# Feed-forward blocks that prepare their input early, in a third buffer, beside causal attention on one NeuronCore

## The chip, the cores and the metric

One core of a Trainium2 chip runs the whole program. Its engines are TensorE (PE in the profile, with its weight loads shown apart as PEld), VectorE (DVE), ScalarE (ACT), GpSimd (POOL) and SyncE (SP), which here only issues DMAs. The metric is the device time of one execution in microseconds. Three runs of the kernel before gave a median of 2549.21 us (2546.5 to 2558.14).

## The reference

The input is x of 4096 tokens by 256 features. A causal attention with 16 heads of 16 features works on the normalised and scaled x; its output is added to x and normalised again, which gives x1. Then x1 goes through a feed-forward network with ternary weights (times a scale for each output feature), and the sum of both is normalised once more.

```python
def _L0_ffn_ref(x, w1_w, w1_s, w2_w, w2_s, h1_w, h1_s, h2_w, h2_s, w3_w, w3_s):
    h = jax.nn.silu(_tlin(x, w1_w, w1_s)) * _tlin(x, w2_w, w2_s)   # 256 -> 1024
    h = jax.nn.gelu(_tlin(h, h1_w, h1_s), approximate=False)       # 1024 -> 1024
    h = jax.nn.gelu(_tlin(h, h2_w, h2_s), approximate=False)       # 1024 -> 1024
    return _tlin(h, w3_w, w3_s)                                    # 1024 -> 256
x = L0_attn_x
x = _layernorm(x + _L0_attn_ref(x, L0_attn_gamma, L0_attn_beta, L0_attn_w_qkv))
x = _layernorm(x + _L0_ffn_ref(x, ...))
```

## The kernel before

The 4096 tokens are eight blocks of 512. First come the projections of q, k and v. Then the attention runs over query blocks in the order 0, 1, 2, 3, 4, 6, 7, 5 and, inside each, over four groups of four heads. Every group has two passes over the key blocks. The pass of maxima (`row_max`) multiplies q and k on TensorE (line 411, with the causal mask added by line 418 on the diagonal block) into a two-bank PSUM tile `s`, and VectorE reduces each tile to row maxima (line 422). The pass of scores multiplies again (line 455), ScalarE takes the exponential (line 459), GpSimd zeroes the upper triangle of the diagonal block (line 462), and TensorE multiplies with v into `opsum` (line 473). Both passes share three buffers of `s`.

The feed-forward part of a block ("feed", line 677) starts when the attention of that block is in DRAM, and two feeds, one in each of two slots, are cut into pieces that a hand-written planner (`other`, line 551) puts between the attention's instructions. One call of `other` is a tick of `self.clock`; a tick may give one piece of TensorE work and one deferred step (a "chore": a vector, scalar or GpSimd step of a feed, in one queue, first in, first out). The order of TensorE's instructions is the order in which the planner emits them; the other engines' instructions are ordered by the scheduler of the language. A feed has these stages:

- start (line 643): x is loaded into the slot's own buffer `x1`, the attention's output into the one buffer `at`; GpSimd adds them (line 653), and a layer norm follows in six steps: statistics on VectorE (lines 130 and 131), the inverse root on GpSimd (135, 136), a small product on VectorE (139) and four applications on ScalarE (143).
- transposes of x1 (line 729) and the split of x1 into a high and a low part.
- the gated stage: for each of eight output chunks, two groups of four matmuls (line 748) into the PSUM tile `m`, of which there is one bank. After the first group ScalarE copies it out scaled, `u` (line 751), takes tanh of `u` (753), and VectorE forms (tanh + 1) * u (754). After the second group VectorE multiplies with it (756) and GpSimd splits the result into two parts (700, 701).
- two hidden stages of eight chunks (line 776). ScalarE copies each chunk out into four `raw` buffers (794). At the end of a stage all four get Gelu in one go (705), because the exponential and Gelu need different function tables; for that time the attention does maxima only (`hold`, `saving`). Then GpSimd splits `raw`, two chunks in each chore.
- the last product (line 818), scaled by VectorE into `ys`, which takes the buffer `at` (line 824); GpSimd adds x1 (831), the layer norm follows, and SP writes the block out (834).

Two locks, `at` and `raw`, keep the feeds from holding these buffers at the same time: `at` is taken from the start until x1 is made, and again from the last product until the output is written.

When the attention has ended (line 597 on), what is left of the other feeds runs first. Then comes block 5, the last, alone (the "tail"): eight PSUM banks, splits on VectorE instead of GpSimd, Gelu straight from PSUM (788), and a check that each weight is unchanged by its conversion (`inspect`, line 673), for which SP loads every weight tile again. Its attention never goes to DRAM first: it lies in `final`, and line 649 adds it to x into `at`.

Of the kernel before, what the change touches and what calls it, by code (L numbers as in the profile page):

```python
# [7 lines left out]
F32 = mybir.dt.float32  # L8
FR = mybir.dt.float32r
AF = mybir.ActivationFunctionType  # L10
ALU = mybir.AluOpType
# [36 lines left out]
class Layer:  # L48
# [33 lines left out]
    def run(self):  # L82
        tc, nc, a = self.tc, self.nc, self.a
        with ExitStack() as ctx:
            dram = self.pool(ctx, "dram", space=DRAM)
            cst = self.pool(ctx, "cst")
            self.small = self.pool(ctx, "small", 4)
            self.qaug = [dram.tile([H, 48, B], F32, name=f"qaug{b}") for b in range(NB)]
            self.kaug = [dram.tile([H, KR, B], F32, name=f"kaug{b}") for b in range(NB)]
            self.vaug = [dram.tile([NQ, P, 4, 4, D + 1], F32, name=f"vaug{b}") for b in range(NB)]  # L90
            self.attn = [dram.tile([B, E], F32, name=f"attn{b}") for b in range(NB)]

            self.ident = cst.tile([P, P], F32, name="ident")
            make_identity(nc, self.ident)
            self.mhalf = cst.tile([P, 4], F32, name="mhalf")
            nc.gpsimd.memset(self.mhalf, -0.5)
            self.wbad = cst.tile([P, 22], F32, name="wbad")
            self.wseq = (
                [("glu", g, 0) for g in range(4)]
                + [(n, g, k) for n in ("h1T", "h2T") for g in range(4) for k in range(2)]  # L100
                + [("w3T", 0, k) for k in range(2)]
            )
            self.sc = {}
            for n in ("w1_s", "w2_s", "h1_s", "h2_s"):
                self.sc[n] = cst.tile([P, 8], F32, name=n)
            self.w1_half = cst.tile([P, 8], F32, name="w1_half")
            self.s3 = cst.tile([P, E], F32, name="s3")

            with ExitStack() as fctx, self.in_order(mybir.EngineType.PE):
                self.layer(fctx)  # L110
            bad = self.verdict(cst)
            with tc.If(bad > 0), ExitStack() as gctx:
                self.general(gctx)

    def scales(self):
        for n, t in self.sc.items():
            self.nc.sync.dma_start(t, self.a[n].rearrange("(c p) -> p c", p=P))
        self.nc.gpsimd.tensor_scalar(self.w1_half, self.sc["w1_s"], 0.5, None, ALU.mult)
        s3 = self.a["w3_s"].rearrange("(o f) -> o f", o=1)
        self.nc.sync.dma_start(self.s3, s3.broadcast_to([P, E]))  # L120

    def norm_steps(self, dst, src):
# [18 lines left out]
        def apply(ts):  # L141
# [4 lines left out]
            lambda: stats((0, 1)), lambda: stats((2, 3)), scale, shift, lambda: apply((0, 1)), lambda: apply((2, 3)),  # L146
        )

    def layernorm(self, dst, src):
        for step in self.norm_steps(dst, src):  # L150
            step()

    def defer(self, fn, delay=0, patience=None):

        if self.tail:
            return fn()
        self.asked += 1
        self.chores.append([delay, patience, fn])

    def chore(self, ripe):  # L160
        if self.chores:
            c = self.chores[0]
            if c[0] > 0:
                c[0] -= 1
            elif c[1] is None or ripe or c[1] <= 0:
                self.chores.pop(0)
                c[2]()
                self.did += 1
            else:
                c[1] -= 1  # L170

    def settle(self):

        goal = self.asked
        while self.did < goal and not self.tail:
            yield None, True

    def take(self, what):

        while self.busy[what] and not self.tail:  # L180
            yield None, True
        self.busy[what] = True

    def free(self, what):
        self.busy[what] = False
# [94 lines left out]
    def layer(self, ctx):  # L280
# [22 lines left out]
        self.chores = []  # L303
        self.asked = self.did = 0
        self.busy = {"at": False, "raw": False}
# [8 lines left out]
        def piece():  # L314
# [8 lines left out]
            for _ in range(SLOTS):  # L323
                if not slots[turn] and queue and queue[0] in finished:
                    slots[turn] = self.feed(queue.pop(0), turn)
# [7 lines left out]
            return None, True  # L333

# [134 lines left out]
        def product(qb, qd, kb, t, first, last, pt):  # L469
# [10 lines left out]
            nc.scalar.copy(osb, opsum)  # L480

            def divide():
# [6 lines left out]
                if qb == ORDER[-1]:  # L489
                    if qd == 0:  # L490
                        self.final = self.fk.tile([P, 4, E], F32, name="final")
# [59 lines left out]
        def other():  # L551

            self.clock += 1
            self.chore(len(pending) >= KEEP)
# [42 lines left out]
        spare = next((i for i in range(SLOTS) if not slots[i]), None)  # L597
        if spare is not None:
            self.loaded = self.load(ORDER[-1], spare)
            self.wtiles[spare] = []  # L600
            self.weights(spare, 2)
# [4 lines left out]
        while queue or any(slots):  # L606
            self.clock += 1
            self.chore(True)
            piece()
        if spare is None:  # L610
            spare = 0
            self.loaded = self.load(ORDER[-1], spare)
            self.wtiles[spare] = []
# [5 lines left out]
        for _ in self.feed(ORDER[-1], spare):  # L619
            pass  # L620
# [17 lines left out]
    def load(self, b, slot):  # L638
        x1 = self.fk.tile([P, 4, E], F32, name=f"x1{slot}")
        self.nc.sync.dma_start(x1, tokens(self.a["x"][b * B : (b + 1) * B]))  # L640
        return x1

    def start(self, b, slot, here=False):

        nc, fk = self.nc, self.fk
        x1 = self.loaded if here else self.load(b, slot)
        at = fk.tile([P, 4, E], F32, name="at")
        if here:
            nc.vector.tensor_tensor(at, x1, self.final, ALU.add)
            nc.sync.dma_start(tokens(self.attn[b]), self.final)  # L650
        else:
            nc.sync.dma_start(at, tokens(self.attn[b]))
            self.defer(lambda: nc.gpsimd.tensor_tensor(at, x1, at, ALU.add), 3)
        for step in self.norm_steps(x1, at):
            self.defer(step)
        return x1

# [19 lines left out]
    def feed(self, b, slot):  # L677
# [3 lines left out]
        if not self.tail:  # L681
            self.wtiles[slot] = []

# [27 lines left out]
        def parted(r, h, i):  # L711
            for c in (2 * i, 2 * i + 1):
                split(r[:, c % 2], *(x[:, c % 4] for x in h[c // 4]))
# [4 lines left out]
        yield from self.take("at")  # L718
        x1 = self.start(b, slot, self.tail)
        self.weights(slot, 2)  # L720
        yield from self.settle()
        self.free("at")
        yield from pause(1)
# [13 lines left out]
        for c in range(8):  # L737
# [4 lines left out]
            for i in range(2):  # L742
# [6 lines left out]
                if i == 0:  # L749
                    u = ft.tile([P, B], F32, name="u", bufs=1)  # L750
                    nc.scalar.activation(u, s, AF.Identity, scale=self.w1_half[:, c : c + 1])
                    th = ft.tile([P, B], F32, name="th")
                    nc.scalar.activation(th, u, AF.Tanh)
                    nc.vector.scalar_tensor_tensor(th, th, 1.0, u, ALU.add, ALU.mult)  # L754
                else:
                    nc.vector.scalar_tensor_tensor(th, s, sc["w2_s"][:, c : c + 1], th, ALU.mult, ALU.mult)  # L756
                    split(th, *(x[:, c % 4] for x in h[-1]))
                yield spent(4 * MM, True)
            if self.tail and c % 2:
                self.inspect(c // 2, wt)  # L760
        yield from pause(2)

        for j, sn in ((4, "h1_s"), (12, "h2_s")):
            parts, h = h, []
            yield from self.take("raw")
            if not self.tail:
                raw = [self.fa.tile([P, 2, B], F32, name=f"raw{i}", bufs=1) for i in range(4)]
            for c in range(8):
                g = j + 2 * (c // 2)
# [3 lines left out]
                for k in range(8):  # L773
                    hi, lo = parts[k // 4]
# [6 lines left out]
                if self.tail:  # L781
# [5 lines left out]
                    th = ft.tile([P, B], F32, name="th")  # L787
                    nc.scalar.activation(th, s, AF.Gelu, scale=sc[sn][:, c : c + 1])
                    split(th, *(x[:, c % 4] for x in h[-1]))
                else:  # L790
# [4 lines left out]
                    if c == 7:  # L795
                        self.saving += 1
                        h = [pair(), pair()]
                        self.defer(lambda: gelu(raw), 0, PATIENCE)
                        for i in range(4):
                            self.defer(lambda i=i: parted(raw[i], h, i))  # L800
                yield spent(8 * MM, True)
            if not self.tail:
                self.weights(slot, g + 5)
                yield from self.settle()
            self.free("raw")
            yield from pause(3)

        yield from self.take("at")
        ys = fk.tile([P, 4, E], F32, name="at")
        wts = self.weights(slot, 22)[20:]  # L810
        for u in range(2):
            yp = bank().rearrange("p (t e) -> p t e", e=E)
            for t in range(2):
# [10 lines left out]
            nc.vector.tensor_tensor(  # L824
                ys[:, 2 * u : 2 * u + 2], yp, self.s3.unsqueeze(1).to_broadcast([P, 2, E]), ALU.mult
            )
# [4 lines left out]
        self.defer(lambda: nc.gpsimd.tensor_tensor(ys, ys, x1, ALU.add))  # L831
        for step in self.norm_steps(ys, ys):
            self.defer(step)
        self.defer(lambda: nc.sync.dma_start(tokens(a["out"][b * B : (b + 1) * B]), ys))
        yield from self.settle()
        self.free("at")

    def general(self, ctx):
# [21 lines left out]
        for b in range(NB):  # L860
            x1 = self.start(b, 0)
# [82 lines left out]
```

## Time and profile before

| | |
|---|---|
| median of three runs | 2549.21 us (2546.5 to 2558.14) |
| the profiled execution | 2551.3 us; its span from first to last instruction 2549.6 us |
| PE busy | 2276.0 us, 89% of the span |
| DVE, ACT, POOL busy | 1546.8, 1427.2, 701.6 us |
| mean granted TensorE clock | 0.922 of full speed |
| first feed's transposes / end of the attention / block 5 alone until the end | about 290 us / 2390 us / 2549.6 us |

A row of a group of instructions gives the source line, engine, operation, what it writes and reads with shape and count, then total busy time and mean duration, and then the engine's idle time just before them with what ended it. In a timeline each row is one instruction or a run of equal ones, with start and duration in us; a bracket at its end is the idle time of the engine before it and what ended that. In a list of waits the three numbers are the total in us, how often, and the longest.

### The profile page before, as it was taken

What the parts mean: (1) busy time and instruction counts of PE and PEld (TensorE: products, weight loads), DVE (VectorE), ACT (ScalarE), POOL (GpSimd) and SP (SyncE); (2) the same over time, 40 slices, a digit from 0 to 9 for tenths busy, and PEclk for the clock granted to TensorE, in tenths of its full rate; (3) what the DMA queues carried; (4) which work ended last, traced back from release to release, by engine and by line L of the source; (5) the groups of instructions that cost most, each with busy time, mean ns of one, the idle gap of its engine ahead of it and who ended that gap; (6) DMA issues with size and microseconds to landing.
All of it is one profiled execution on the core that took longest, in us unless ns stands there. A gap on an engine that the chain in (4) does not pass through costs nothing.

```text
span 2549.6 us, 36265 instructions
## 1 busy us (share of the span) xinstructions
PE 2276.0 (89%) x13986; PEld 1222.3 (48%) x13986; DVE 1546.8 (61%) x1795; ACT 1427.2 (56%) x1764; POOL 701.6 (28%) x1008
## 2 busy tenths in 40 slices
PE   4877899998988989999998989999998999999686
PEld 3645345454554543544554534444554534544265
DVE  3544777666757557677656568677655468661263
ACT  3332656555655557556566657666555677667521
POOL 3333222223322134132304033232224132131211
PEclk8777979998998989989999989999999999999888
DMA  7766634533453434534444534444444443443265
GB/s 196 203 162 166 166 101 117 125 105 94 111 135 102 117 99 125 119 88 114 116 120 125 112 85 133 119 111 111 121 109 116 114 128 94 109 111 85 75 169 138
DMA packets 250707, 308.97 MB, mean 121 GB/s; under 512 B 41248, under 2 KB 178592, under 8 KB 250528
## 3 DMA queue, kind: packets, MB, share of 16 engines
q1 hardware_dynamic: 141904, 184.87, 25.3%
q0 software_dynamic: 107264, 119.86, 21.4%
q8 instruction: 113, 1.85, 0.3%
q10 hardware_dynamic: 1360, 1.84, 0.2%
q14 instruction: 66, 0.54, 0.1%
HBM read 267.41 MB, written 38.54 MB: 120 GB/s over the span
## 4 chain that ended last, share of the span: by engine, by line
PE 65%; DVE 13%; issue 6%; ACT 6%; DMA 5%; POOL 5%; SPq 1%; POOLq 0%; ACTq 0%; DVEq 0%
PE m L776 18%; PE opsum L473 16%; PE s L455 11%; PE s L411 10%; DVE mp L422 10%; PE m L748 3%; ACT p L459 3%; PE m L818 2%; PE s L418 1%; PE s L245 1%; POOL act L701 1%; DMA qt<-hl 1%; DVE st L130 1%; DVE th L754 1%; POOL wt L634 1%
## 5 line engine op out<-in xcount | busy, mean ns | idle before, releaser
L422 DVE TENSOR_REDUCE mp<-s 128x2 f32<-128x1024 f32 (+3 forms) x1152 | 1269.0, 1132 | 613.8 <-PE s L411 462.2
L459 ACT ACTIVATE p<-s 128x1024 f32<-128x1024 f32 (+3 forms) x1152 | 1062.7, 955 | 660.1 <-PE s L455 647.6
L455 PE MATMUL s<-qt,sk 50*128 50x512 f32 (+3 forms) x2304 | 514.0, 454 | 83.9 <-DVE mp L422 45.5
L473 PE MATMUL opsum<-p,vk 128*17 128x512 f32 (+3 forms) x4608 | 561.7, 590 | 18.4 <-POOL p L462 13.5
L411 PE MATMUL s<-mk,qt 48*128 48x512 f32 (+3 forms) x2304 | 516.9, 449 | 66.0 <-DVE mp L422 30.8
L776 PE MATMUL m<-act,wt 128*128 128x512 f32 x1792 | 482.7, 412 | 0.2 <-DVE th L756 0.2
L455 PEld LDWEIGHTS s<-qt,sk 50*128 50x128 f32 x2304 | 223.8, 194 | 399.3 <-DVE mp L422 148.8
L776 PEld LDWEIGHTS m<-act,wt 128*128 128x128 f32 x1792 | 324.8, 191 | 126.7 <-issue 54.9
L411 PEld LDWEIGHTS s<-mk,qt 48*128 48x128 f32 x2304 | 230.3, 197 | 319.6 <-ACT p L459 115.1
L473 PEld LDWEIGHTS opsum<-p,vk 128*17 128x17 f32 x4608 | 98.6, 98 | 251.4 <-issue 216.5
L462 POOL TENSOR_SCALAR_AFFINE_SELECT p<-p 128x256 f32<-128x256 f32 x256 | 105.0, 419 | 300.6 <-ACT p L459 299.5
L634 POOL DMA_DIRECT2D wt<-h2T_in x64 | 48.2, 752 | 429.8 <-PE m L776 337.0
L634 POOL DMA_DIRECT2D wt<-h1T_in x64 | 48.9, 764 | 361.8 <-PE m L776 233.0
L701 POOL TENSOR_TENSOR act<-raw,act 128x512 fp32r<-128x512 f32 x112 | 140.1, 1270 | 0.0
L794 ACT ACTIVATE raw<-m,h_s 128x512 f32<-128x512 f32 x112 | 77.1, 688 | 105.1 <-PE m L776 105.1
L748 PE MATMUL m<-xh,wt 128*128 128x512 f32 x224 | 103.2, 461 | 10.3 <-DVE th L756 10.1
L418 PEld LDWEIGHTS s<-tri,pick 64*128 64x128 f32 x1024 | 97.3, 206 | 6.9
L748 PE MATMUL m<-xl,wt 128*128 128x512 f32 x224 | 91.4, 408 | 0.0
L418 PE MATMUL s<-tri,pick 64*128 64x128 f32 (+1 forms) x1024 | 88.8, 252 | 0.0
L776 PE MATMUL bank<-act,wt 128*128 128x512 f32 x256 | 70.3, 432 | 16.2 <-DMA wt<-h2T_in 7.2
L700 POOL CAST act<-raw 128x512 fp32r<-128x512 f32 x112 | 65.2, 609 | 55.6 <-ACT raw L705 55.6
L700 POOL CAST act<-th 128x512 fp32r<-128x512 f32 x56 | 34.3, 613 | 140.5 <-DVE th L756 140.4
(116 smaller groups left out, 1529.9 us busy)
## 6 DMA issues: line engine op xcount, KB each, us to landing
mk<-kaug SPq DMA_DIRECT2D x288, 200.0 KB
sk<-kaug SPq DMA_DIRECT2D x288, 200.0 KB
wt<-h1T_in POOLq DMA_DIRECT2D x64, 512.0 KB, 4.1
wt<-h2T_in POOLq DMA_DIRECT2D x64, 512.0 KB, 5.1
vk<-vaug SPq DMA_DIRECT2D x144, 136.0 KB
qt<-qaug SPq DMA_DIRECT2D x64, 192.0 KB
wt<-w1T_in POOLq DMA_DIRECT2D x32, 256.0 KB, 3.6
wt<-w2T_in POOLq DMA_DIRECT2D x32, 256.0 KB, 5.0
```

The lines of the kernel that those rows point to most:

```text
L411: nc.tensor.matmul(m[:, e, :k1], qt[rows, r, t * P : (t + 1) * P], kt[rows, r, :k1], start=True, stop=kb != qb,)
L418: nc.tensor.matmul(m[:, e, k1 - P + half * i : k1], pick[rows, i], tri[rows, : P - half * i], start=False, stop=i == 1,)
L422: nc.vector.tensor_reduce(mp[:, r, :, t, kb], m[:, :, :k1], AX.X, ALU.max)
L455: nc.tensor.matmul(s[:, e, lo:], kt[rows, r, t * P : (t + 1) * P], qt[rows, r, lo:], start=True, stop=True)
L459: nc.scalar.activation(p[:, :, lo:], s[:, :, lo:], AF.Exp, scale=0.25)
L462: nc.gpsimd.affine_select(out=p[:, :, lo : lo + P], in_=p[:, :, lo : lo + P], compare_op=ALU.is_ge, fill=0.0, base=0, pattern=[[0, 2], [1, ...
L473: nc.tensor.matmul(opsum[32 * j : 32 * j + D + 1, lo:], vt[:, t, j], pt[j // 2][:, j % 2, lo:], start=first, stop=last,)
L634: self.nc.gpsimd.dma_start(dst, src)
L700: eng.tensor_copy(hi, src)
L701: eng.tensor_tensor(lo, src, hi.bitcast(F32), ALU.subtract)
L748: nc.tensor.matmul(s, wt[:, 2 * i + k, cols], x[:, k], start=k == n == 0, stop=k == n == 1)
L776: nc.tensor.matmul(s, wts[k // 4][:, k % 4, cols], x[:, k % 4], start=k == n == 0, stop=k == 7 and n == 1)
```

## The change

Six edits, mostly to the feeds.

1. x1 is made before the feed has a slot. Three buffers of `x1` rotate. A new step `prepare`, called at every tick, starts the next block (`start`) as soon as its attention is there, fewer than three `x1` are in use and `at` is free. The sum is made in place in `x1` by a chore that waits seven ticks, after which `at` is free again; the norm's first and fourth step wait two ticks more each. A slot takes the block when all of this has been emitted.
2. Tanh reads PSUM directly, with the scale folded in; `u` is gone. VectorE's (tanh + 1) * product reads the product from PSUM, and the factor that `u` carried is in a new constant `w12`.
3. Chores are in lanes: one for the next block's preparation and one for each slot. A tick still does one chore, but each lane counts its own delays.
4. The locks `raw0` to `raw3` replace one lock on `raw`; each is freed when its own split is done. A split chore handles one chunk instead of two. The second hidden stage starts when half of the splits have been emitted. The lock `x` covers the split of x1 from the transposes to the end of the gated stage.
5. The last product's two halves are scaled into buffers of `th` (three instead of two) and added to x1 by GpSimd half by half; the norm and the output work in place in `x1`. A slot that is done loads the first two weight tiles of its next block at once.
6. For block 5, `final` is the buffer `at`, and sum and norm (`finish`) are emitted ahead of the tail.

```diff
-    def defer(self, fn, delay=0, patience=None):
+    def defer(self, lane, fn, delay=0, patience=None):
...
+        names = list(self.lanes)
+        turn = self.clock % len(names)
+        for name in names[turn:] + names[:turn]:
...
+            elif done:
+                continue
...
+        def prepare():
+
+            if not project and not self.next and queue and queue[0] in finished and self.live < 3:
+                if "at" not in self.busy:
+                    b = queue.pop(0)
+                    self.next = b, self.start(b)
+            self.more = bool(queue or self.next)
...
-            nc.scalar.copy(osb, opsum)
+            (nc.vector.tensor_copy if self.hold else nc.scalar.copy)(osb, opsum)
...
-    def load(self, b, slot):
-        x1 = self.fk.tile([P, 4, E], F32, name=f"x1{slot}")
+    def load(self, b):
+        self.live += 1
+        x1 = self.fk.tile([P, 4, E], F32, name="x1", bufs=3)
...
+        def total():
+            nc.gpsimd.tensor_tensor(x1, x1, at, ALU.add)
+            self.free("at")
+
+        self.defer("next", total, 7)
+        for delay, step in self.norm_steps(x1, x1):
+            self.defer("next", step, delay)
         return x1
+
+    def reserve(self, slot):
+
+        self.spare = slot
+        self.loaded = self.load(ORDER[-1])
+        self.weights(slot, 2)
+
+    def finish(self):
+
+        self.nc.vector.tensor_tensor(self.loaded, self.loaded, self.final, ALU.add)
+        self.nc.sync.dma_start(tokens(self.attn[ORDER[-1]]), self.final)
+        self.layernorm(self.loaded, self.loaded)
...
-                    u = ft.tile([P, B], F32, name="u", bufs=1)
-                    nc.scalar.activation(u, s, AF.Identity, scale=self.w1_half[:, c : c + 1])
-                    th = ft.tile([P, B], F32, name="th")
-                    nc.scalar.activation(th, u, AF.Tanh)
-                    nc.vector.scalar_tensor_tensor(th, th, 1.0, u, ALU.add, ALU.mult)
+                    th = ft.tile([P, B], F32, name="th", bufs=3)
+                    nc.scalar.activation(th, s, AF.Tanh, scale=self.w1_half[:, c : c + 1])
+                    nc.vector.scalar_tensor_tensor(th, th, 1.0, s, ALU.add, ALU.mult)
                 else:
-                    nc.vector.scalar_tensor_tensor(th, s, sc["w2_s"][:, c : c + 1], th, ALU.mult, ALU.mult)
+                    nc.vector.scalar_tensor_tensor(th, s, self.w12[:, c : c + 1], th, ALU.mult, ALU.mult)
...
-            yield from self.take("raw")
...
+                if not self.tail and c % 2 == 0:
+                    yield from self.take(f"raw{c // 2}")
...
+                    if k % 4 == 0 and c == 0 and j == 12:
+                        yield from self.settle(slot, 4 - k)
...
-                        for i in range(4):
-                            self.defer(lambda i=i: parted(raw[i], h, i))
+                        for i in range(8):
+                            self.defer(slot, lambda i=i, raw=raw, h=h: parted(raw[i // 2][:, i % 2], h, i))
...
-            nc.vector.tensor_tensor(
-                ys[:, 2 * u : 2 * u + 2], yp, self.s3.unsqueeze(1).to_broadcast([P, 2, E]), ALU.mult
-            )
+            ys = ft.tile([P, 2, E], F32, name="th", bufs=3)
+            nc.vector.tensor_tensor(ys, yp, self.s3.unsqueeze(1).to_broadcast([P, 2, E]), ALU.mult)
+            half = x1[:, 2 * u : 2 * u + 2]
+            nc.gpsimd.tensor_tensor(half, half, ys, ALU.add)
...
-        self.defer(lambda: nc.gpsimd.tensor_tensor(ys, ys, x1, ALU.add))
-        for step in self.norm_steps(ys, ys):
-            self.defer(step)
-        self.defer(lambda: nc.sync.dma_start(tokens(a["out"][b * B : (b + 1) * B]), ys))
-        yield from self.settle()
-        self.free("at")
+        for delay, step in self.norm_steps(x1, x1):
+            self.defer(slot, step, delay)
...
+        if self.more:
+            self.weights(slot, 2)
+        elif self.spare is None:
+            self.reserve(slot)
```

## The prediction

> **What bounds the kernel now.** I read the shares first, then the stretches, the waits, and the places on the timeline where those waits stand. TensorE is busy for 2276.0 of 2549.6 us. After the projections (250 us) come two stretches: the attention with the feeds in it, and the tail. Columns: the stretch and its length, busy time of PE, PEld, DVE, ACT and POOL with counts, granted clock, DMA share, GB/s.
>
> ```profile
> 250.00:2390.00 2140.00, 1997.30 (x12567) 1011.79 (x12567) 1357.45 (x1446) 1316.74 (x1577) 589.12 (x815) 0.94 0.45 113
> 2390.00:2549.60 159.60, 108.60 (x462) 84.59 (x462) 76.77 (x148) 29.32 (x46) 23.37 (x28) 0.83 0.50 141
> ```
>
> The middle stretch is TensorE's: 1997.3 of 2140 us, at a clock of 0.94. The matmuls of attention and feeds stay the same in number, so in that stretch the change can only work on the 142.7 us in which TensorE stands, and on the clock. In the tail it stands for 51 us. These are the waits of the middle stretch that the edits touch (total us, times, longest):
>
> ```profile
> PE s L455 <- DVE mp L422: 45.0, 77, 5.9
> PE s L411 <- DVE mp L422: 28.4, 43, 6.8
> PE opsum L473 <- POOL p L462: 13.5, 5, 4.8
> PE m L748 <- DVE th L756: 10.1, 11, 6.1
> DVE st L130 <- POOL at L653: 15.9, 5, 9.9
> DVE st L130 <- POOL at L831: 15.1, 5, 6.8
> ```
>
> "PE waits for line 422" is one name for several things. VectorE works in order, so a reduction is late whenever VectorE stood at something else. The last two rows are such cases: a layer norm's statistics wait for GpSimd's sum, the reductions queue up behind them, the three buffers of `s` fill, and TensorE stops. The two longest on the timeline (start, duration; in the bracket the idle time before it and what ended it):
>
> ```profile
> 722.00 2.34 POOL L653 TENSOR_TENSOR at<-x,at 128x1024 f32<-128x1024 f32 x1 [11.21 <-DMA at<-attn]
> 724.38 0.43 DVE L130 BATCH_NORM_STATS2 st<-at 128x6 f32<-128x256 f32 x1 [9.92 <-POOL at L653]
> 725.72 0.79 PE L455 MATMUL s<-qt,sk 50*128 50x512 f32 x2 [5.87 <-DVE mp L422]
> ...
> 1952.51 2.36 POOL L831 TENSOR_TENSOR at<-at,x 128x1024 f32<-128x1024 f32 x1
> 1954.90 0.75 DVE L130 BATCH_NORM_STATS2 st<-at 128x6 f32<-128x256 f32 x2 [6.78 <-POOL at L831]
> 1956.83 0.80 PE L411 MATMUL s<-mk,qt 48*128 48x512 f32 x2 [6.76 <-DVE mp L422]
> ```
>
> The reader is to see the chain from GpSimd through VectorE to TensorE: 9.92 us on VectorE, of which the buffers absorb four, cost TensorE 5.87. Two more such stalls, at 952.73 and 1386.34, cost 2.32 and 2.72 us, both after a sum of line 831.
>
> **The change, part by part.** Reference is the median, 2549.2 us; the durations come from the execution with a span of 2549.6 (2551.3 with what lies around it), so a difference read from it is taken off the median as it is, without scaling.
>
> (a) *Early x1, half adds.* At a start, the seven ticks put the sum well behind its loads and two more put the statistics behind the sum, so the stall of 5.87 us goes. At an end, one add of 2.37 us becomes two halves (1.27 us by line 701, a GpSimd operation of half the size), the first while the second half is still being multiplied. But the built instruction order leaves only zero to two reductions between a half's scaling and its statistics, so VectorE still waits there: of 6.76 + 2.32 + 2.72 us I keep about 4. Total 5.87 + 11.8 = 17.67, less 4: −13.7. After the two long stalls the clock falls, as it does after a third (next part):
>
> ```profile
> 726.00:730.00 4.00, 3.64 (x14) 2.58 (x14) 3.59 (x10) 2.17 (x3) 1.27 (x2) 0.50 0.82 229
> 1957.00:1961.00 4.00, 4.00 (x12) 2.64 (x12) 2.06 (x6) 2.56 (x5) 1.27 (x2) 0.56 0.55 168
> 631.50:636.00 4.50, 4.50 (x16) 1.75 (x16) 1.74 (x2) 1.69 (x3) 2.29 (x3) 0.50 0.01 4
> ```
>
> Four microseconds at half speed are two lost, so two long stalls carry 4 more, of which I take 3. **(a) −17**, between −22 (all of it) and 0 (what is late next takes it: the reductions behind the half adds).
>
> (b) *The product (tanh + 1) * u.* One of 64 took ten times its time:
>
> ```profile
> 623.05 6.59 DVE L754 SCALAR_TENSOR_TENSOR th<-th,u 128x512 f32<-128x512 f32 x1
> 631.49 0.80 PE L748 MATMUL m<-xh,wt 128*128 128x512 f32 x1 [6.09 <-DVE th L756]
> ...
> L754 DVE SCALAR_TENSOR_TENSOR th<-th,u 128x512 f32<-128x512 f32 x64 | 52.0, 813 | 15.5 <-ACT th L753 14.9
> L756 DVE SCALAR_TENSOR_TENSOR th<-m,w_s,th 128x512 f32<-128x512 f32 x56 | 41.8, 746 | 13.8 <-PE m L748 12.8
> ```
>
> Its median is 691 ns; in those 6.59 us GpSimd's splits ran back to back. Line 756, with one input in PSUM, never took over 752 ns. The Trainium skill (SBUF — State Buffer, "Who interferes with whom") says that a VectorE instruction with both inputs in SBUF contends with a GpSimd instruction that reads SBUF, and one with at most one such input does not. By the rule the new product, with one input in PSUM, can't be caught: −6.1, and −2 for the slow clock after it. By the rows alone one event in 64 may have another cause and come again: 0. I take the rule, since the only form that was caught has two SBUF inputs. **(b) −8**, between −8 and 0.
>
> (c) *No `u`.* 56 activations of 688 ns (line 751) leave ScalarE, 38.5 of its 1316.7 us, 2.9%. In the same list TensorE's waits on `p` are 13.2 us (line 411) and 12.9 (line 455), together 26.1; 2.9% of them is 0.8. What hides the rest is that ScalarE mostly waits for TensorE. **(c) −1**, between −3 and 0.
>
> (d) *The bank `m` is held longer.* Before, it was free after `u`, 0.69 us. Now tanh reads it (no row has tanh from PSUM; nearest is Gelu from PSUM with a scale, 688 ns, so 0.69), then VectorE's product reads it too (0.75, by line 756), with two handovers of about 0.05: 1.54 us, plus VectorE's queue. VectorE is busy for 63% of the stretch, mostly with reductions of 1.22 us; half of one, 0.61 × 0.63 = 0.39. In the built order 26 of the 56 chunks have their second group only four to six attention matmuls behind the first, some 1.3 us of cover. So 1.54 + 0.39 − 1.30 = 0.63 us for each, 26 × 0.63 = 16; elsewhere the cover is long. A third of it shortens stalls that would follow at `s` anyway. **(d) +10**. The bounds: 0, since the bank can't be free earlier than before, and +54 (first rival). What waits behind the second group of line 748 on TensorE is the attention, and for that the reductions and exponentials. The rule of the Trainium skill that speaks against this edit (Perfetto Trace Analysis, "Matmuls") is that independent groups of matmuls should rotate through PSUM banks, so that emptying one overlaps the next group. One bank can't rotate; before, 0.69 us of emptying fitted under 1.3 us of other matmuls, and the row that says so is the 10.1 us of waits at line 748, 6.1 of them from (b). By the rule in full the term is +46, by the rows +10.
>
> (e) *Splits of one chunk.* The same GpSimd work in twice as many steps. A mask (line 462) that falls behind a block of splits stops TensorE for 4.83 us at 922.96 and 4.38 at 1494.26, most of the 13.5 above. The built order puts blocks of splits inside a diagonal four times where it was three. **(e) +5**, between 0 and +7.
>
> (f) *SP's queue.* It is in order. A load of `at` behind a store of the same block waits for its landing: three times before, five times after, some 4.7 us each. Behind it stand weights, and loads of `k` issued early. **(f) 0**, at most +5 if a weight is late once.
>
> (g) *The rest.* Two more weight tiles (34 of the gated stage's for 32) are four DMAs of 0.74 us of issue, at a DMA share of 0.45; three copies of `osb` go to VectorE; the new product is 0.06 us longer, 56 × 0.06 = 3 us. VectorE's 37% of idle time hides this; uncovered it costs those 3 us. Lanes and locks: the same 14 Gelu events (3.9 us each) and 46 function-table loads in both orders, so **(g) 0**.
>
> (h) *The tail.*
>
> ```profile
> 2411.48 1.23 DVE L649 TENSOR_TENSOR at<-x,final 128x1024 f32<-128x1024 f32 x1 [5.23 <-DMA out<-at]
> 2416.82 2.80 PE L729 MATMUL bank<-ident,x 128*128 128x128 f32 x8 [17.15 <-ACT x L143]
> ```
>
> Block 5's sum waits for `at` until block 7's output has been stored. After the change it does not wait, but it shares VectorE and ScalarE with block 7's norm: two checks of weights (1.31 us each) and four applications stand ahead of its own. By that order the transposes come about 5 us earlier. The end gains 1.9 us: the add of 2.33 us after the last product becomes two halves, the first of them beside the product. The hidden stages in between are paced by weights, and two fewer checks stand in the gated stage: −1. **(h) −8**, between −12 and −2.
>
> Sum: −17 − 8 − 1 + 10 + 5 + 0 + 0 − 8 = −19, so **2530 us**.
>
> **The rivals.** *The bank becomes the bound (slower).* If in the 26 short chunks the product stands behind a whole reduction, each costs 1.54 + 1.22 − 1.30 = 1.46 us, 38 in all; behind half of one and another, 1.54 + 0.61 + 1.22 − 1.30 = 2.07, 54. The other terms sum to −29, so the middle, +46, gives 2566. It turns slower above 29 / 26 = 1.1 us for each chunk, and measurably above 1.6. For it: a reduction is queued whenever TensorE runs ahead; against it: the pass of scores has none.
>
> *The stalls move (no change).* VectorE waits for half adds as it did for whole ones, a start's statistics meet the second lane's steps, and (a) and (b) give 5 instead of 25: −5 − 1 + 10 + 5 − 8 = +1, with less of (d), since TensorE then stands at `s` anyway: about 2546. For it: the zero to two reductions of cover in the built order.
>
> *Everything works (larger gain).* (a) −22, (b) −8, (c) −3, (d) +4, (e) 0, (h) −12: −41, 2508. Against it: (e)'s fourth block is there in the order.
>
> **How the numbers follow.** A measurement of this kernel tells about 0.5% (12.7 us) from no change: 2536.5 and 2562. The main case has 0.42 and a range of its own of 2518 to 2540, a tenth of it above 2536.5; larger gain 0.14; no change 0.22; the bank 0.22, nearly all above 2562. Faster 0.38 + 0.14 = 0.52, same 0.04 + 0.22 = 0.26, slower 0.22. The range leaves out the lower third of the larger gain (0.05) and the upper half of the bank's case (0.11): 2504 to 2566.
>
> **What would show it.** (a) The waits of statistics on the sum at a start vanish, those on half adds stay under 2 us each, and TensorE's waits for line 422 fall from 73 to about 55 us. (b) The longest (tanh + 1) * product takes under 1 us. (d) A new wait of `m` at the gated matmuls for that product, 10 to 16 us in all; above 29 the bank decides. (e) Waits of `opsum` for the mask rise to about 18. (h) The transposes of block 5 start near 21 us after the attention's end instead of 26. The prediction is wrong if TensorE's idle time from 250 us on to the attention's end does not fall by about 11 us, or if it falls and the granted clock takes it back.

## The result and the profile after

Over twenty executions of each kernel, the changed kernel takes 2547.26 us (median) and the kernel before 2552.01. The ratio is 0.9982, with an interval from 0.9964 to 1.0001: no change that the measurement can tell. The forecast was 2530 us, a ratio of 0.9925. The time lies within the stated range, but the gain that was the likeliest case did not come.

The profiled execution has a span of 2545.2 us at a mean granted clock of 0.926 (before 2549.6 at 0.922). Its two later stretches, in the columns of the forecast's table (stretch and length, busy time of PE, PEld, DVE, ACT, POOL, granted clock, DMA share, GB/s):

```profile
250.00:2390.00 2140.00, 1983.90 (x12459) 1011.93 (x12459) 1348.14 (x1446) 1274.21 (x1505) 582.45 (x809) 0.94 0.45 112
2390.00:2545.00 155.00, 113.23 (x538) 83.16 (x536) 76.23 (x149) 34.24 (x48) 30.75 (x37) 0.91 0.56 153
```

In the first of them TensorE is busy for 13.4 us less than before. That is no gain: by 2390 us it has 108 fewer matmuls behind it. Cut at the marks of the program instead of at fixed times (first matmul of a maxima pass, last product of scores and v, end), the two executions compare so:

| | before | changed |
|---|---|---|
| up to the first maxima matmul | 63.0 us | 59.0 |
| attention, from there to its last product | 2326.0 | 2341.7 |
| TensorE without work in the attention | 185.7 | 206.8 |
| of it, from 250 us on | 142.3 | 156.1 |
| tail, from there to the end | 160.6 | 144.5 |
| of it, up to block 5's transposes | 27.8 | 21.9 |

So the attention became 15.7 us longer (its end comes 11.7 us later, since it began 4.0 us earlier) and the tail 16.1 us shorter. The waits of the attention in the changed kernel (250 to 2390 us; total us, times, longest) show the first:

```profile
PE s L479 <- DVE mp L446: 46.0, 60, 7.9
DVE st L132 <- POOL x L863: 32.0, 9, 8.5
PE s L435 <- DVE mp L446: 26.0, 40, 5.3
DVE st L132 <- POOL x L679: 16.9, 4, 8.0
PE m L786 <- DVE th L790: 14.1, 19, 1.4
PE opsum L497 <- POOL p L486: 11.3, 4, 5.0
```

Line 446 is the old 422, and 132 the old 130. The statistics' waits for GpSimd were to shrink. At the ends (line 863, the half adds) they grew from 15.1 to 32.0 us, and at the starts (line 679) they stayed: 16.9 for 15.9. TensorE's idle gaps over 0.3 us next to a norm's statistics (from 3 us before them to 8 after, from 250 us on) add up to 49.9 us, where they were 32.3.

This is the longest of the ends on the timeline:

```profile
1655.49 2.54 POOL L739 TENSOR_TENSOR act<-raw,act 128x512 fp32r<-128x512 f32 x2
1656.12 0.68 DVE L861 TENSOR_TENSOR th<-m,s 128x512 f32<-128x512 f32 x1
...
1662.67 2.50 POOL L739 TENSOR_TENSOR act<-raw,act 128x512 fp32r<-128x512 f32 x2
1665.12 1.28 POOL L863 TENSOR_TENSOR x<-x,th 128x512 f32<-128x512 f32 x1
1666.43 0.76 DVE L132 BATCH_NORM_STATS2 st<-x 128x6 f32<-128x256 f32 x2 [8.50 <-POOL x L863]
1668.57 0.79 PE L479 MATMUL s<-qt,sk 50*128 50x512 f32 x2 [7.66 <-DVE mp L446]
```

The first half is scaled by 1656.8. Its add is next in GpSimd's queue behind the splits of the second hidden stage, which run without a pause until 1665.1. The statistics stand on VectorE one reduction behind the scaling. They wait 8.5 us, and the reductions behind them wait too. TensorE stands for 7.66 us.

And this is a start:

```profile
810.69 0.38 SPq L523 DMA_DIRECT2D attn<-ao  x1
814.68 0.38 SPq L676 DMA_DIRECT2D at<-attn  x1
819.93 2.34 POOL L679 TENSOR_TENSOR x<-x,at 128x1024 f32<-128x1024 f32 x1 [3.53 <-DMA at<-attn]
822.30 0.43 DVE L132 BATCH_NORM_STATS2 st<-x 128x6 f32<-128x256 f32 x1 [7.96 <-POOL x L679]
823.91 0.80 PE L479 MATMUL s<-qt,sk 50*128 50x512 f32 x2 [4.72 <-DVE mp L446]
```

Since a block is now started as soon as its attention is there, its load follows the last store of the same data. It is issued 4.0 us after the store, lands 5.2 us later, the add takes 2.3, and the statistics have been first in VectorE's queue for 8 us. One of the longest stalls lies ahead of 250 us, where neither the forecast nor the lists of waits look. It is the start of the first feed, and it was there before as well (9.85 us on VectorE, 8.29 on TensorE):

```profile
235.18 0.75 DVE L132 BATCH_NORM_STATS2 st<-x 128x6 f32<-128x256 f32 x2 [9.06 <-POOL x L679]
238.13 1.22 PE L259 MATMUL s<-xh,wh 128*128 128x512 f32 x2 [7.49 <-DVE kl L265]
```

After each of these stalls the clock is down, as it was before. The first row is the window behind the start at 814.68 us, the second that behind the end; the last two show how long it stays down:

```profile
824.00:828.00 4.00, 4.00 (x11) 2.52 (x12) 3.57 (x9) 1.94 (x2) 0.23 (x1) 0.50 0.00 2
1668.60:1672.60 4.00, 4.00 (x13) 1.81 (x14) 3.55 (x4) 2.64 (x3) 0.00 (x0) 0.50 0.07 11
823.90:829.60 5.70, 5.69 (x16) 3.39 (x16) 3.83 (x10) 1.96 (x3) 1.28 (x2) 0.50 0.00 1
1668.60:1676.10 7.50, 7.50 (x28) 5.09 (x28) 4.72 (x4) 3.07 (x3) 1.33 (x2) 0.50 0.18 55
```

At half speed these 5.7 and 7.5 us lose 2.9 and 3.8 us, where the forecast had counted 2 for a stall.

### The profile page after: what moved, and what is told of

Its sections match the earlier page's. It is cut to its first block, busy times and chain, and to the rows that moved or that the text cites. A ratio compares the mean times of both kernels' runs of the same rounds, so it can differ in the third digit from the quotient of the medians.

```text
span 2545.2 us, 36334 instructions
## 1 busy us (share of the span) xinstructions
PE 2263.3 (89%) x13986; PEld 1218.5 (48%) x13986; DVE 1540.0 (61%) x1800; ACT 1389.4 (55%) x1695; POOL 706.4 (28%) x1021
## 5 line engine op out<-in xcount | busy, mean ns | idle before, releaser
L497 PE MATMUL opsum<-p,vk 128*17 128x512 f32 (+3 forms) x4608 | 559.5, 587 | 11.9 <-POOL p L486 11.3
L786 PE MATMUL m<-xh,wt 128*128 128x512 f32 x224 | 103.9, 464 | 15.7 <-DVE th L790 14.1
L816 PE MATMUL bank<-act,wt 128*128 128x512 f32 x256 | 65.2, 411 | 15.2 <-DMA wt<-h2T_in 6.7
```

The lines of the kernel that those rows point to most:

```text
L497: nc.tensor.matmul(opsum[32 * j : 32 * j + D + 1, lo:], vt[:, t, j], pt[j // 2][:, j % 2, lo:], start=first, stop=last,)
L786: nc.tensor.matmul(s, wt[:, 2 * i + k, cols], x[:, k], start=k == n == 0, stop=k == n == 1)
L816: nc.tensor.matmul(s, wts[k // 4][:, k % 4, cols], x[:, k % 4], start=k == n == 0, stop=k == 7 and n == 1)
```

## The experiments

Each ratio is to the kernel before on the same chip; the runs were made on three chips, so ratios are compared and not times.

The theory after reading the trace: the seven ticks and the two ticks are counted where the planner emits, but only TensorE's order follows the emission. VectorE's order is the scheduler's, and it has the statistics too early for GpSimd's queue and the loads' landing. (In the built program none to two reductions stand between the scaling of an end's half and the next statistics on VectorE. With four or eight further ticks ahead of the statistics the number is the same; with the order of the first run below it is 5 to 18.) The rival: TensorE would stand at `s` anyway, and the stalls would only move.

### Statistics kept behind the reductions emitted before them

`after` records an order of two instructions and adds no semaphore between them; `pin` is true for the norms in question. In the first run it holds for the norm at the end of a block, in the second for that of a start, in the third for both. TensorE's order and every instruction stay the same.

```diff
                         nc.vector.tensor_reduce(mp[:, r, :, t, kb], m[:, :, :k1], AX.X, ALU.max)
+                        self.reduced = nc.cur_bb.bb.instructions[-1].name
...
                 nc.vector.bn_stats(st, src[:, t])
+                if pin and not self.tail:
+                    self.after(nc.cur_bb.bb.instructions[-1], self.reduced)
```

> The changed kernel, with one ordering added: the statistics of a block's last norm may not stand on VectorE ahead of the reductions that were emitted before them (the instructions and TensorE's order stay the same). Theory, early place: the stalls of TensorE come from statistics that VectorE's order has too early, ahead of a half add that stands behind GpSimd's splits. Then the waits of statistics on half adds (32 us between 250 and 2390) fall below 8, the stalls of 7.94, 7.66 and 4.48 us go, three slow-clock spells of about 2 us with them, and the ratio to the kernel before is 0.990 (about 2526 us; 0.987 to 0.993). Rival, the stalls only move: TensorE would stand at s anyway for another reason, idle time stays, and the ratio stays at 0.997 to 0.999.

> The changed kernel, with the same ordering for the statistics of x1's norm at a start alone. Early place: the waits of statistics on the sum (16.9 us) fall below 4, the stalls of 4.72 and 5.28 us and two slow-clock spells go: ratio 0.993 (0.991 to 0.996), about 2535 us. The stalls only move: 0.997 to 0.999.

> The changed kernel, with both orderings. Early place: the two gains add, TensorE's idle time in the attention falls by 30 us, and the ratio is 0.985 (0.981 to 0.989), about 2514 us. The stalls only move: 0.995 to 0.999, and the waits for the reductions show another cause ahead of them.

Measured: 0.9855 (0.9833 to 0.9877) for the ends, 0.9931 (0.9910 to 0.9952) for the starts, 0.9768 (0.9744 to 0.9791) for both: 2496.4 us. The end that was shown above, in the first run:

```profile
1654.73 0.68 DVE L864 TENSOR_TENSOR th<-m,s 128x512 f32<-128x512 f32 x1
...
1663.77 1.28 POOL L866 TENSOR_TENSOR x<-x,th 128x512 f32<-128x512 f32 x1
...
1678.86 0.74 DVE L132 BATCH_NORM_STATS2 st<-x 128x6 f32<-128x256 f32 x2
```

The add still starts 8.4 us after the scaling, but the statistics come 14 us after its end and wait for nothing. With both orders the waits of the attention are these:

```profile
PE s L482 <- DVE mp L448: 29.3, 64, 1.7
PE s L437 <- DVE mp L448: 16.0, 36, 0.6
DVE st L132 <- POOL x L866: 3.5, 2, 2.1
```

TensorE waits for reductions as often as in the changed kernel, but never over 1.7 us. The stall of the first feed's start is gone too. The rival falls: little took the place of the stalls. What did are waits for masks (`opsum`), 19.6 us for 11.3 in the changed kernel, the longest of them 5.6 us just behind where the first start had stalled. The starts gained what was expected, the ends and both together more. In the profiles the attention goes from 2341.7 to 2285.3 us; 35.5 of these 56.4 are idle time (206.8 to 171.3), and the other 20.9 are busy time of the same matmuls. I summed what the clock withholds, (1 − granted clock) × 4 us over windows of 4 us, from 250 us to the end of the attention: 117.7 us before, 126.3 in the changed kernel, 109.2 with the ends ordered and 97.2 with both. So in these profiles the clock withholds 29 us less without the stalls, 23 of them while TensorE is busy. The last section says how far that holds for other executions.

### The same order in the kernel before

The same lines in the kernel before, with two ticks more ahead of each norm's first statistics.

> The kernel before, with both orderings of the statistics added and two ticks of delay ahead of the first statistics of each norm. Early place: the kernel before has the same fault in a smaller size (31 us of waits of statistics in the attention, stalls of 5.87, 6.76, 2.32, 2.72 us and two slow-clock spells); they go, and the ratio is 0.991 (0.987 to 0.994). Rival, its order was late enough and only its rare stalls matter: 0.996 to 1.000. The distance between this and the changed kernel with both orderings (0.977) is what the change is worth once the order is right: by the forecast's other terms (early x1 aside) 0.998 of it, or about 0.4%; by the measured 2.3% more, if making x1 early is itself worth something.

0.9951 (0.9937 to 0.9965). The waits of statistics fall to one of 2.5 us, and TensorE's for the reductions have no stall over 2.2:

```profile
PE s L458 <- DVE mp L424: 35.3, 79, 0.9
PE s L413 <- DVE mp L424: 25.7, 50, 2.2
DVE st L130 <- POOL at L834: 2.5, 1, 2.5
```

The fault was there before, at half the price that I expected. With the order right in both, the change is worth 0.9768 / 0.9951 = 0.982, or 1.8%; the changed kernel as it is loses nearly all of that in its norms. TensorE's waits for masks are 19.7 us here.

### One more step ordered

The small product `mr` of each norm, which waits for GpSimd's inverse root, is kept behind the reductions as well.

```diff
             nc.vector.scalar_tensor_tensor(mr[:, :, 0], mv[:, :, 0], -1.0, rs[:, :, 0], ALU.mult, ALU.mult)
+            if pin and not self.tail:
+                self.after(nc.cur_bb.bb.instructions[-1], self.reduced)
```

> The changed kernel with both orderings, and the small product of each norm (mr, which waits 17.4 us for GpSimd's inverse root) ordered behind the reductions too. Early place for every step that waits on GpSimd: the waits fall below 5 us and the ratio is 0.974 (against 0.977). Rival, waits of at most 2.4 us are covered by the three buffers of s: 0.976 to 0.978.

0.9775 (0.9752 to 0.9798). The waits of `mr` fall from 17.4 to 2.4 us in all and the time stays: waits of VectorE up to 2.4 us cost TensorE nothing that can be measured here.

### Is it GpSimd's queue?

The half adds go to VectorE, and nothing is ordered.

```diff
-            nc.gpsimd.tensor_tensor(half, half, ys, ALU.add)
+            nc.vector.tensor_tensor(half, half, ys, ALU.add)
```

> The changed kernel with the half adds on VectorE instead of GpSimd, nothing ordered. Early place behind GpSimd's splits: an add on VectorE has no splits ahead of it, the waits on half adds go, and the ratio is near that of the first ordering: 0.988 (0.984 to 0.993), if an add takes about 0.7 us. Contention: the add has two SBUF inputs and meets the splits, takes 2 us or more each time and up to 6.6, and the ratio is 0.992 to 0.998. If the splits were not the cause, 0.998.

0.9853 (0.9823 to 0.9883), as much as ordering the ends gave. Mean of the adds and their idle time:

```profile
L863 DVE TENSOR_TENSOR x<-x,th 128x512 f32<-128x512 f32 x16 | 13.4, 835 | 0.3
```

Their median is 692 ns, the longest 1857. So it was the splits ahead of the adds; what contention there was between these adds, with both inputs in SBUF, and GpSimd cost little. With both orders as well:

> The changed kernel with both orderings and the half adds on VectorE. If an ordering behind the reductions already covers the splits, moving the adds gains nothing: 0.977 (0.975 to 0.979). If GpSimd's queue still holds something up (masks behind the adds), 0.973 to 0.975.

0.9813 (0.9794 to 0.9832). No gain on top, as expected if the order already covers the splits. It is slower than 0.9768, with idle time in the attention of 173.1 us against 171.3. By the granted clock of all executions the difference is the clock's: (1 − granted clock) × span has a mean of 168 us here and 158 with the orders alone, and what is left of the span is 2335 us in both. Why the clock differs isn't shown; the two ran on different chips.

### Half adds alone

The kernel before with the half adds and nothing else.

```diff
+            half = ys[:, 2 * u : 2 * u + 2]
+            nc.gpsimd.tensor_tensor(half, half, x1[:, 2 * u : 2 * u + 2], ALU.add)
...
-        self.defer(lambda: nc.gpsimd.tensor_tensor(ys, ys, x1, ALU.add))
```

> The kernel before with the half adds of part 5 alone: each half of the last product is added to x1 by GpSimd as soon as it is scaled, no deferred sum, nothing ordered. Theory, half adds stand early behind GpSimd's splits and the statistics go early with them: the waits of statistics on the sums at an end (15.1 us in the attention) rise to 25 to 35, TensorE's idle time by 8 to 15 us with 2 us of slow clock for each long stall, ratio 1.005 (1.002 to 1.009). The forecast's step (a) for the ends (about -8 us): 0.997. No effect: 0.999 to 1.001.

1.0005 (0.9994 to 1.0017), and the waits at the ends went down, from 15.1 to 11.5 us:

```profile
DVE st L130 <- POOL at L828: 11.5, 7, 5.7
```

The expectation fails: half adds by themselves don't make the fault. TensorE's idle time from 250 us on rose by 3.7 us (142.3 to 146.0), where 8 to 15 were expected. I compared when the first halves come, from the start of the last Gelu of either feed to the start of the scaling. In the kernel before with half adds that is 10.2 to 87.6 us, and the adds start 0.1 to 1.8 us after the scaling. In the changed kernel it is 17.5, 8.2, 3.6, 3.6, 5.9 and 25.9 us, and the adds start 0.1, 4.5, 8.3, 8.3, 6.3 and 0.1 us after the scaling. The splits follow each Gelu at once and take GpSimd 8 × (0.61 + 1.27) = 15 us. A half add comes late where the last product falls into these 15 us, which in the changed kernel it does four times in six.

### The last product later

So I moved the product and left the order alone.

```diff
         yield from self.settle(slot)
+        yield from pause(5)
         wts = self.weights(slot, 22)[20:]
```

> The changed kernel with one line more: a feed pauses five ticks before its last product, so that the splits have left GpSimd's queue when the half adds come. Nothing is ordered; TensorE's order changes with the pause. In the changed kernel four of six first halves are scaled 3.6 to 8.2 us after the last Gelu, with 4 to 8 us of splits ahead of their add; with half adds alone they came 10 us or more after it and waited at most 1.8. If the meeting of last product and splits is what makes the ends stall: first adds start within 2 us of their scaling, the waits of statistics on half adds fall from 32 to below 12 us, and the ratio is 0.990 (0.986 to 0.994), less what the feeds lose by starting later. If the early place alone is, the waits stay above 20 us and the ratio near 0.998.

0.9885 (0.9857 to 0.9913), 2521.2 us. Six of seven first halves now come 11 us or more after the last Gelu, by the same measure, with adds that start within 0.8 us. One comes 6.9 us after it, and its add starts 5.1 us late. In the built program the statistics stand as close behind the scaling as without the pause, one or two reductions. The waits at the ends and at the starts:

```profile
DVE st L132 <- POOL x L864: 12.7, 10, 4.1
DVE st L132 <- POOL x L679: 12.0, 4, 5.5
```

The first is a little over the 12 that were expected. It takes both: a half add that goes out at once, and a last product that comes while splits are in GpSimd's queue. What brings the product so close to Gelu was not tried. It can be the lanes, the locks by tile or the splits of one chunk, and also that the last product no longer waits three ticks and for the lock `at`, which the kernel before with half adds still does.

### Tanh from PSUM, alone, undone, and undone with the order right

In the kernel before, part 2 alone; in the changed kernel, and in the one with both orders, part 2 undone (with two buffers of `th`, for room).

```diff
-                    th = ft.tile([P, B], F32, name="th", bufs=3)
-                    nc.scalar.activation(th, s, AF.Tanh, scale=self.w1_half[:, c : c + 1])
-                    nc.vector.scalar_tensor_tensor(th, th, 1.0, s, ALU.add, ALU.mult)
+                    u = ft.tile([P, B], F32, name="u", bufs=1)
+                    nc.scalar.activation(u, s, AF.Identity, scale=self.w1_half[:, c : c + 1])
+                    th = ft.tile([P, B], F32, name="th", bufs=2)
+                    nc.scalar.activation(th, u, AF.Tanh)
+                    nc.vector.scalar_tensor_tensor(th, th, 1.0, u, ALU.add, ALU.mult)
```

> The kernel before with part 2 alone: tanh and the product read PSUM, no u. By the forecast's terms (bank held longer +10, contended product -8, ScalarE -1) the ratio is 1.000 (0.996 to 1.004), the waits of the gated matmuls for the product are 12 to 16 us, and no product takes over 1 us. If the longer hold outweighs the rest, 1.004 to 1.014; if the contention does, 0.993 to 0.996.

> The changed kernel with part 2 undone: u is copied out again, tanh and the product read u, and th has two buffers instead of three to make room. By the forecast's terms (bank held longer +10, the contended product -8, ScalarE -1) undoing is worth about 0: ratio 0.998 (0.994 to 1.002); the waits of the gated matmuls for the product (14 us) fall below 5, and a product over 2 us shows up once or twice. If the longer hold of the bank is the larger term, the ratio falls to 0.993 or lower; if the contention is, it rises to 1.002 or more.

> The changed kernel with both orderings, and part 2 undone (u kept, two buffers of th). It asks what part 2 is worth once the norms no longer stall TensorE. Bank hold exposed: the 15 us of waits at the gated matmuls are no longer hidden by later stalls, so that taking them away gains, 0.972 to 0.975 against 0.977 with part 2. Part 2 worth what it was alone in the kernel before (0.4%): 0.981. No matter: 0.976 to 0.978.

Alone it gains: 0.9959 (0.9943 to 0.9975). Undone in the changed kernel, 0.9993 (0.9975 to 1.0010), which can't be told from 0.9982. Undone with both orders, 0.9852 (0.9828 to 0.9876): slower than 0.9768, by 0.9%, and than the 0.9813 of the same chip (with its half adds on VectorE) by 0.4%. The row of the new product in the first run:

```profile
L754 DVE SCALAR_TENSOR_TENSOR th<-th,m 128x512 f32<-128x512 f32 x56 | 38.2, 682 | 22.4 <-ACT th L753 22.2
```

All 56 take about 0.68 us. In each of the five profiles with `u` one product or more took over 2.8 us, the longest 6.59 (before), 6.51, 6.11, 2.90 and 2.83; in the nine without `u` none of 64 took over 0.69. The waits of the gated matmuls for this product are there too, 10.0 us in 19 (14.1 in the changed kernel), and go with `u` (3.0 are left, all for the second product). Yet the attention's idle time is the same with part 2 alone (185.9 us for 185.7), and with both orders it is smaller with `u` (164.6 for 171.3) while the time is longer. So the waits at the bank do not decide. The granted clock of all executions says in what form the gain comes. (1 − granted clock) × span has a mean of 191 us with part 2 alone and 203 in the kernel before on the same chip; with both orders it is 168 (half adds on VectorE) and, with `u`, 177 on the same chip. These 11 and 9 us are nearly the whole gain in mean span, 11 and 10 us. Part 2 shows in the tail as well (next section, under (h)); why the clock is granted more stays open.

## Why the prediction was wrong

**(a) is the step that failed.** It has two sentences that the trace contradicts. "The seven ticks put the sum well behind its loads and two more put the statistics behind the sum": they do so in the planner's emission, which binds TensorE alone. A load that follows the store of its block stands in (f), "some 4.7 us each", and was put at 0; at a start the statistics wait for it. And the sentence on the two halves' adds, 1.27 us each and the first beside the second half's product, left out what stands ahead of them in GpSimd's queue. I had asked what moves past SP's queue, and not what the half adds move behind on GpSimd. Forecast −17. In the profiles it is +17.6 us of idle time next to statistics, and the stall of the first start stayed as well (7.5 us for 8.3). The sign that the prediction had named came: from 250 us to the attention's end TensorE's idle time was to fall by about 11 us, and it rose by 13.8. The clock's share of a stall was too small, too, at 2 us for 2.9 and 3.8. The mechanism itself, statistics that hold up reductions, was right: taking it away is worth 2.1% of the changed kernel's time.

**(b), (c), (d).** No product was caught, as (b) had said, and every profile with `u` has one that was; what that is worth in time no run tells apart. The waits at the bank are 14.1 us at most 1.4 long, within the forecast's 10 to 16, so (d) has the right size as a wait. As a sum, −8 − 1 + 10 = +1 was wrong for part 2 alone: its gain is 0.41% of 2554, 10 us. (c) counted ScalarE's work in the attention and left out the tail, see (h). The rule against it, about rotating banks, named a real wait that wasn't decisive; the bank rival is excluded for this kernel.

**(e)** was forecast +5. The waits of `opsum` for masks fell from 13.5 to 11.3 us, and those for splits fell from 4.3 to 0.4. With both orders the masks are at 19.6 us, near the 18 of the forecast, but at 19.7 in the kernel before with the orders as well. So no run shows that the splits of one chunk cost anything.

**(h)** was forecast −8 and is −16.1. The transposes come 5.9 us earlier (5 forecast) and the end after TensorE's last instruction is 1.9 shorter, as forecast. The last product's part is 2.2 shorter. The hidden stages were taken to be paced by weights, with −1 for two fewer checks of weights in the gated stage; from the last gated matmul to their own last they take 80.3 us for 86.3. The 20 us where they begin, before:

```profile
2436.00:2456.00 20.00, 13.68 (x35) 8.63 (x34) 14.11 (x25) 5.93 (x8) 1.48 (x2) 0.66 0.45 130
```

and after the change:

```profile
2442.00:2462.00 20.00, 15.13 (x55) 10.92 (x54) 14.00 (x25) 3.58 (x5) 2.24 (x3) 0.91 0.72 197
```

In the hidden stages TensorE waited 6.3 us for splits on VectorE before and 3.4 after, and at their beginning the clock was at 0.66 before. The two fewer checks do not explain that; the step that (h) left out is part 2. The five profiled kernels that keep `u` take 85.9 to 89.0 us for the hidden stages, at 0.66 in the first 20 us. The one of 89.0 us is the changed kernel with part 2 undone, which has all the rest of the change:

```profile
2441.75:2461.75 20.00, 13.49 (x36) 8.47 (x35) 12.69 (x22) 6.40 (x9) 1.69 (x3) 0.66 0.44 124
```

The nine without `u` take 79.6 to 83.7 us, at 0.74 to 0.91; with part 2 alone it is 83.2 at 0.74. In the tail's gated stage `u`, which has one buffer, can't be written again until VectorE's product has read it. These are ScalarE's waits for that around this stage (total us, times, longest), in the kernel before and in the changed one with `u`:

```profile
ACT u L751 <- DVE th L754: 10.5, 6, 2.1
ACT u L789 <- DVE th L792: 10.6, 6, 2.5
```

Without `u` that wait is gone, and the last gated splits come sooner. What the rest of the change adds to part 2 here (83.2 to 80.3 us) was not taken apart.

The rival "the stalls move" had the right time, 2546, by luck, and in part the right place: VectorE does wait for the half adds. But in it the stalls were to be nearly as large as before; they became larger, and a gain in the tail twice the forecast paid for them.

## What to carry to other kernels

A delay holds only on the engine whose order it sets. Where a scheduler orders the other engines, look in each engine's own order at what stands between a step and the step that feeds it, and in the feeding engine's queue at what stands ahead. If a step on the engine that feeds the bound one waits for another engine, fix its place behind work that is ready; here two such orderings, without one instruction more, were worth 2.1%.

## What the runs showed of the hardware

A stall of TensorE can cost more than its length, since the granted clock is 0.50 for 5.7 and 7.5 us behind the two stalls shown. From the changed kernel's profile to that with both orders, 35.5 us of idle time went, and the busy time of the same matmuls in the attention fell from 2134.9 to 2114.0 us. But one execution is one sample of it: the kernel with `mr` ordered too has the same median and about the same idle time (169.1 us), and its profiled execution has 112.6 us withheld for 97.2. Over all executions (1 − granted clock) × span has a mean of 181 us in the changed kernel (20 executions), 158 with both orders (6) and 170 with `mr` ordered too (5), so taking the stalls away gave back some 11 to 22 us of clock (on different chips; one execution of a kernel differs from the next by about 10). About 100 us were withheld in the attention even where no norm stalled, and what takes them was not looked into.

VectorE's product with both inputs in SBUF took 2.8 to 6.6 us at its longest in each of five profiles, beside a median of 0.69. With one input in PSUM none took over 0.69 us in nine profiles. The half adds on VectorE, again with both inputs in SBUF, took up to 1.86 us.
